# Second layers ahead of slot 3's sums, both transposes ahead of slot 5's placements, and loads of x early in a turn of a graph layer

## The chip, the cores and the metric

The kernel runs on one core of one Trainium2 chip. The metric is the device time of one execution in microseconds (us). The engines have their own instruction lists and meet through semaphores: PE (TensorE, matrix products; PEld is its weight load), DVE (VectorE), ACT (ScalarE), POOL (GpSimd) and SP (SyncE, which here only issues DMA transfers). Each engine works its list in the order in which it is written.

## The reference

One layer of a graph network on 12500 nodes with 128 features and 412500 edges with 48 attributes, whose receivers `dst` are sorted. All in float32.

```python
h   = max(layernorm(x), 0)                          # 12500 x 128
agg = segment_sum(edge_attr_48, dst, 12500)         # 12500 x 48
u   = graph_globals[0]                              # one row, the same for each node
hid = relu(concat([h, agg, u], axis=1) @ W1 + b1)   # 12500 x 256
out = x + hid @ W2 + b2                             # 12500 x 128
```

## The kernel before

The edges come in twelve turns of 33792 edges (and a rest), eleven groups of four chunks of 768 edges each. The groups of a turn lie in six slots of buffers `e0` to `e5` (`SLOTS`: two groups in a slot, one in slot 4). In the same turn 1024 nodes are worked on, as two blocks A and B of 512 (indices 0 and 1).

The steps, by the names in the code:

- Sums (`sums`, names `su0` to `su5`, L804): for each chunk PE multiplies the edges' attributes by a one-hot matrix `oh` that DVE makes from the receivers (`onehots`, L748). Results go to the PSUM banks `S0` (slots 0, 2, 4) and `S1` (slots 1, 3, 5). ACT copies them out (`ss0` to `ss5`, L808). So slot 5's sums may begin only when `ss3` has read `S1`.
- Placements (`place`, `pc0` to `pc4`, L826; `place_ends`, `pc5`, L788): PE adds a group's sums to the windows of the banks `ax` and `ay`, with one-hot matrices `pl`, `pln`, `plf` from DVE (L754, L767).
- Norm: DVE makes statistics of x for A and B (`stats`, L834) and the variance (`variance`, L839 to L844), ACT the root (`root`, L848), DVE its reciprocal and the shift (`shift`, L853 and L854), ACT the normed x (`norm`, four pieces a block, `xn0.0` to `xn1.3`, L860).
- Turn of a block (`turn`, `tu0` and `tu1`, L869): PE transposes the normed block into the bank `pt` or `po`; ACT copies it to `hta` or `htb` (`hT0`, `hT1`, L870).
- First layer (`layer_x` L879, `layer_e` L884, four products each), and `relu` on ACT (L889) into `hida` and `hidb`. It stands at the end of a turn.
- Second layer (`second`, `w20` for A and `w21` for B, L910; before, six of B's eight products stand apart as `second_begun`, L904). It works in the next turn on what `relu` left. Then DVE adds x and b2 into the output held in SBUF (`ho0`, `ho1`, L914; `hold`), and makes x + b2 of the present block (`add_b`, L864).
- Loads: e by SP (`load_e`), x by ACT (`load_x`), which refills the one buffer of a block for the next turn. The held outputs are stored at the end of the kernel.

The order of the work is written out by hand in `body`; each engine's list is that order, restricted to the engine. `Flow.order` finds the waits from what each step reads and writes. On PE the first turn skips the second layers, which have no input yet (`f.brief`): PE then waits for the weights and raises the semaphores of the skipped steps. PE's loop of code is cut at `f.mark`.

Of the kernel before, what the change touches and what calls it, by code (L numbers as in the profile page):

```python
# [18 lines left out]
P = 128  # L19
# [7 lines left out]
IN = 1024  # L27
BN = 512
R = 4
# [452 lines left out]
def kernel(  # L482
# [18 lines left out]
    NIT = E // IE  # L501
# [18 lines left out]
    def bank(name):  # L520
        return psum.tile([P, BN], F32, name=name)
# [4 lines left out]
    ph = [bank("ph0"), bank("ph1")]  # L526
    po = bank("po")
# [65 lines left out]
    f = Flow(nc, tc)  # L593
    op = f.op
    A, B, Z = 0, 1, 2
# [37 lines left out]
    def rows_of(ap, i, a, m, r):  # L633
        return span(ap, i, a, m * r).rearrange("(p r) d -> p (r d)", r=r)

    def load_x(k, a, m=P, eng="ACT"):
        r = RR[k]
        dv = xt[k].rearrange("p r d -> p (r d)")
        q = m - m % 16
        dma(eng, f"lx{k}", [], [f"x{k}"], dv[:q], lambda i: rows_of(x, i, a, q, r))  # L640
        if q < m:
            dma(eng, f"lx{k}t", [], [f"x{k}t"], dv[q:m], lambda i: rows_of(x, i, lambda i: a(i) + q * r, m - q, r))
# [78 lines left out]
    def cols(ap, i, a, n):  # L721
        return ap[:, ds(a(i), n)] if not isinstance(i, int) else ap[:, a(i):a(i) + n]
# [33 lines left out]
    def onehots(s):  # L756
        g = SLOTS[s]
        onehot(s, oh[s], ["rel_i"], rel_i[:, g[0] - 1:g[0]] if len(g) == 1 else rel_i[:, g[0] - 1:g[1]:g[1] - g[0]])
# [16 lines left out]
    def place_ends(sides):  # L775

        todo = []
        for side in sides:
            sv, pv, some = ((ss[5], pln, near), (ssf, plf, far_))[side]
            c = 0  # L780
            for j, frm, w, bk, at in some:
                todo.append((-w, side, sv[:, j], pv[:, c:c + w], bk, at, w))
                c += w
        todo.sort(key=lambda v: (v[0], 1 - v[1]))
        fresh = sides == (1,)
        op("PE", "pc5" + "f" * fresh, [v for side in sides for v in (("ss5", "pln"), ("ssf", "plf"))[side]],
           [f"bk{b}" for b in sorted({v[4] for v in todo})], lambda i: [
            nc.tensor.matmul(agg[bk][HI * bk:HI * bk + DE, at:at + w], sv, pv, start=fresh and n == 0, stop=True, skip_group_check=True)  # L788
            for n, (_, _, sv, pv, bk, at, w) in enumerate(todo)], late={"ss5": 1} if 0 in sides else None)
# [24 lines left out]
    def place(s, fresh=(), part=None):  # L814

        groups, sv, pv = SLOTS[s], ss[s], pl[s]
        todo = [(n, j) + v for j, g in enumerate(groups) for n, v in enumerate(pieces(g)) if part is None or v[0] == part]
        todo.sort(key=lambda v: v[2] if len(groups) == 1 else (v[0] if v[1] == 0 else 1 - v[0], v[1]))
        seen = set()

        def emit(i):
            seen.clear()
            out = []
            for _, j, bk, at, frm, w in todo:
                h = HI * bk
                out.append(nc.tensor.matmul(agg[bk][h:h + DE, at:at + w], sv[:, j], pv[:, j, frm:frm + w],  # L826
                                            start=bk in fresh and bk not in seen, stop=True, skip_group_check=True))
                seen.add(bk)
            return out
        op("PE", f"pc{s}" + ("" if part is None else f".{part}"), [f"ss{s}", f"pl{s}"], [f"bk{b}" for b in sorted({v[2] for v in todo})], emit)  # L830

    def stats(k, m=P):
        c = k % 2 * R
        op("DVE", f"st{k}", [f"x{k}", f"x{k}t"], [f"st{k}"], lambda i: [nc.vector.bn_stats(st[k // 2][:m, c + r], xt[k][:m, r]) for r in range(RR[k])])  # L834
# [15 lines left out]
    def shift(n, m=P):  # L850
        s = sm[n][:m]
        f.chain("DVE", f"sh{n}", [f"sm{n}a"], [f"sc{n}", f"sh{n}"],
            lambda: nc.vector.reciprocal(sc[n][:m], sc[n][:m]),  # L853
            lambda: nc.vector.scalar_tensor_tensor(sh[n][:m], s[:, 0], -0.5, sc[n][:m], OP.mult, OP.mult))  # L854

    def norm(k, some, m=P):
        n, c = k // 2, k % 2 * R
        for r in some:
            op("ACT", f"xn{k}.{r}", [f"x{k}", f"x{k}t", f"sc{n}", f"sh{n}"], [f"xn{k}"], lambda i, r=r: [
                nc.scalar.activation(xn[k][:m, r], xt[k][:m, r], AF.Relu, bias=sh[n][:m, c + r:c + r + 1], scale=sc[n][:m, c + r:c + r + 1])])  # L860

    def add_b(k, m=P, eng="DVE"):
        op(eng, f"xb{k}", [f"x{k}", f"x{k}t", "b2"], [f"xb{k}"], lambda i: [
            f.of[eng].tensor_tensor(xb[k][:m], xt[k][:m], b2_sb[:m, None, :].to_broadcast([m, RR[k], D]), OP.add)])  # L864

    def turn(k, m=P, bk=None, key="PT", eng="ACT"):
        pv = (pt if bk is None else bk)[:, :RR[k] * P].rearrange("p (r c) -> p r c", r=RR[k])
        copy = nc.scalar.copy if eng == "ACT" else nc.vector.tensor_copy
        op("PE", f"tu{k}", [f"xn{k}", "ident"], [key], lambda i: [nc.tensor.transpose(pv[:, r, :m], xn[k][:m, r], ident[:m, :m]) for r in range(RR[k])])  # L869
        op(eng, f"hT{k}", [key], [f"hT{k}"], lambda i: [copy(hT[k][:, :, :m], pv[:, :, :m])])  # L870
# [30 lines left out]
    def second_begun(k, bk, key, n):  # L901
        ov = bk.rearrange("p (r d) -> p r d", r=R)
        op("PE", f"w2{k}a", [f"hid{k}.{a}" for a in range(NH)] + ["w2"], [key], lambda i: [
            nc.tensor.matmul(ov[:, r], hid[k][:, a, r], w2[:, a], start=(a == 0), stop=(a == NH - 1)) for r in range(n) for a in range(NH)])  # L904

    def second(k, m=P, bk=None, key="PO", keep=None, begun=0):

        ov = (po if bk is None else bk)[:, :RR[k] * D].rearrange("p (r d) -> p r d", r=RR[k])
        op("PE", f"w2{k}", [f"hid{k}.{a}" for a in range(NH)] + ["w2"], [key], lambda i: [
            nc.tensor.matmul(ov[:m, r], hid[k][:, a, r, :m], w2[:, a], start=(a == 0), stop=(a == NH - 1)) for r in range(begun, RR[k]) for a in range(NH)])  # L910
        if keep is None:
            op("DVE", f"ot{k}", [key, f"xb{k}"], [f"ot{k}"], lambda i: [nc.vector.tensor_tensor(ot[k][:m], ov[:m], xb[k][:m], OP.add)])
        else:
            op("DVE", f"ho{k}", [key, f"xb{k}"] + (["spare"] if k == A else []), [f"hold{k}.{keep(f.at)}"], lambda i: [nc.vector.tensor_tensor(  # L914
                cols(hold[k], i, lambda i: keep(i) * (R * D), R * D).rearrange("p (r d) -> p r d", r=R), ov, xb[k], OP.add)])
# [90 lines left out]
    def body(it):  # L1006
        f.at = it

        def add_slots(*some):
            for s in some:  # L1010
                sums(s)
                if it < NIT - 1:
                    load_e(s, 1)

        keep = lambda i: (i + NIT - 2) % (NIT - 1)
        add_slots(0, 1)
        stats(A)
        farthest()
        fetch(1)
        add_slots(2)  # L1020
        stats(B)
        variance(0, (A, B))
        root(0)
        onehots(0)
        add_slots(3)
        shift(0)
        norm(A, (0,))
        add_slots(4)
        norm(A, (1, 2))
        onehots(1)  # L1030
        add_slots(5)
        norm(A, (3,))
        norm(B, range(R))
        onehots(2)
        onehots(3)
        place(0, (0, 1))
        for s in (1, 2, 3, 4):
            place(s)
        place_ends((0, 1))
        second(A, P, ph[A], "PH0", keep)  # L1040
        add_b(A)
        onehots(4)
        sums_out(A)
        sums_out(B)
        turn(A)
        second_begun(B, ph[B], "PH1", R - 1)
        if it < NIT - 1:
            load_x(A, lambda i: (i + 1) % NIT * IN)
        turn(B, P, po, "PO")
        second(B, P, ph[B], "PH1", keep, R - 1)  # L1050
        add_b(B)
        keep_ends()
        if it < NIT - 1:
            load_x(B, lambda i: (i + 1) % NIT * IN + BN)
        onehots(5)
        places_far()
        fetch_off(1)
        for s in (0, 1, 2, 3, 4):
            places(s)
        places_near()  # L1060
        layers(layer_x)
        layers(layer_e)
        layers(relu)
# [51 lines left out]
    f.at = NIT + 1  # L1115
    ends = [f"ot{k}" for k in range(3)] + [f"x{k}" for k in (A, B)] + [f"hold{k}.{j}" for k in (A, B) for j in range(NIT - 1)]
    op("SP", "end", [], ends, lambda i: [nc.sync.nop(nofuse=True)])
    f.mark, f.half, f.stops = "tu1", "of2", ("su1.b", "su1.c", "su2.b")
    f.brief, f.weights = ("w20", "w21a"), ("lw1h", "lw1a", "lw1b", "lw2")
    f.order((0, NIT - 1))  # L1120
    tc.mark_branch_hint_location("skip", engines=[ET.PE, ET.DVE])
    with tc.tile_critical(no_gpsimd_drain=True):
# [34 lines left out]
```

## Time and profile before

| | |
|---|---|
| device time, median of 3 runs | 259.55 us (259.35 to 259.8) |
| the profiled execution: time / span | 259.39 us / 257.5 us |
| PE busy | 238.0 us (92% of the span) |
| DVE busy | 231.3 us (90%) |
| ACT busy | 129.1 us (50%) |
| share of the chain that ended last: PE / DVE / DMA | 88% / 4% / 3% |
| HBM traffic | 94.33 MB, 366 GB/s over the span |

The span runs from the first to the last instruction. Busy time counts the instructions themselves; waits, branches and the issue of transfers do not count. A matmul of float32 shows as two records. Rows of the timeline begin with start and length in us; a bracket at a row's end names the idle time ahead of it and what ended it. In names, `out<-in` tells what is written and read, without buffer numbers: `s` is `S0` or `S1`, `ss` any of the six copies.

### The profile page before, as it was taken

How to read it: one execution, taken by the hardware profiler on the slowest of the kernel's cores; microseconds unless marked ns; L12 is line 12 of the kernel's file. 1: busy time of each engine (PE TensorE's matmuls, PEld its weight loads, DVE VectorE, ACT ScalarE, POOL GpSimd, SP SyncE). 2: the span in 40 equal slices, each digit the busy share in tenths (PEclk: the TensorE clock that was granted, in tenths of full speed). 3: DMA queues.
4: the chain of work that ended last, by engine and by line, in shares of the span. 5: the costliest groups of instructions: out<-in, count | busy, mean ns of one | idle time of the engine just before them, and what ended most of it. 6: DMA issues, size and time to landing. Idle time of an engine off the chain costs nothing.

```text
span 257.5 us, 17114 instructions
## 1 busy us (share of the span) xinstructions
PE 238.0 (92%) x7539; PEld 187.6 (73%) x7540; DVE 231.3 (90%) x572; ACT 129.1 (50%) x315; POOL 4.5 (2%) x18
## 2 busy tenths in 40 slices
PE   1778499999999999999999999999999999999990
PEld 1668374985976968949949869779589499598680
DVE  6489989989999999999999999999999999999840
ACT  5421273563654735825835646447258358356530
POOL 5000000000000000000000000000000000001000
PEclk9999869999999999999999999999999999999998
DMA  6999999999999999999999999999999999968972
GB/s 201 341 388 386 362 387 392 380 390 393 385 390 393 390 392 391 390 393 387 391 393 389 390 393 389 391 390 390 391 389 390 393 390 391 392 242 313 378 269 65
DMA packets 79508, 94.33 MB, mean 366 GB/s; under 512 B 3227, under 2 KB 72797, under 8 KB 79494
## 3 DMA queue, kind: packets, MB, share of 16 engines
q1 hardware_dynamic: 76086, 88.06, 95.7%
q10 hardware_dynamic: 3312, 6.03, 6.1%
q8 instruction: 7, 0.11, 0.2%
q0 software_dynamic: 96, 0.07, 0.1%
q14 instruction: 7, 0.06, 0.1%
HBM read 87.75 MB, written 6.40 MB: 366 GB/s over the span
## 4 chain that ended last, share of the span: by engine, by line
PE 88%; DVE 4%; DMA 3%; issue 1%; ACT 1%; SPq 0%; ACTq 0%; DVEq 0%
PE s L804 27%; PE ph L910 12%; PE ph L879 8%; PE ax L826 7%; PE ph L904 6%; PE pt L884 5%; PE pt L879 4%; PE ph L884 4%; PE po L879 4%; DMA holda<-in_dst_dram 3%; PE po L869 2%; PE pt L869 2%; PE ax L788 2%; DVE oh L748 1%; DVE pl L754 1%
## 5 line engine op out<-in xcount | busy, mean ns | idle before, releaser
L748 DVE TENSOR_TENSOR oh<-iota_v,rel_i 128x1344 f32<-128x1344 f32 (+1 forms) x78 | 109.7, 1435 | 0.0
L804 PEld LDWEIGHTS s<-e,oh 128*28 128x28 f32 x6336 | 73.3, 109 | 16.5 <-issue 12.0
L804 PE MATMUL s<-e,oh 128*28 128x48 f32 x6336 | 77.0, 210 | 6.1 <-issue 2.5
L889 ACT ACTIVATE hida<-pt,bias 128x512 f32<-128x512 f32 x12 | 8.2, 687 | 50.2 <-PE pt L884 50.2
L860 ACT ACTIVATE xna<-xa,shab,scab 128x128 f32<-128x128 f32 x48 | 23.7, 493 | 13.2 <-DVE shab L854 12.8
L808 ACT COPY ss<-s 128x96 f32<-128x96 f32 (+1 forms) x72 | 16.4, 228 | 24.6 <-PE s L804 24.6
L754 DVE TENSOR_SCALAR pl<-iota_w,off_i 128x186 f32<-128x186 f32 x117 | 27.6, 311 | 0.4
L910 PE MATMUL ph<-w,hida 128*128 128x128 f32 x192 | 24.6, 281 | 0.0
L860 ACT ACTIVATE xnb<-xb,shab,scab 128x128 f32<-128x128 f32 x48 | 23.5, 490 | 1.2
L910 PEld LDWEIGHTS ph<-w,hida 128*128 128x128 f32 x192 | 22.3, 191 | 0.6
L826 PE MATMUL ax<-pl,ss 128*48 128x186 f32 (+1 forms) x120 | 20.9, 324 | 0.0
L826 PE MATMUL ay<-pl,ss 128*48 128x186 f32 (+1 forms) x120 | 20.9, 324 | 0.0
L826 PEld LDWEIGHTS ax<-pl,ss 128*48 128x48 f32 x120 | 14.5, 129 | 4.1
L904 PE MATMUL ph<-w,hidb 128*128 128x128 f32 x132 | 16.5, 275 | 0.0
L904 PEld LDWEIGHTS ph<-w,hidb 128*128 128x128 f32 x132 | 15.6, 192 | 0.0
L826 PEld LDWEIGHTS ay<-pl,ss 128*48 128x48 f32 x120 | 14.5, 129 | 0.0
L884 PE MATMUL pt<-ags,w1a 48*128 48x512 f32 x24 | 13.5, 641 | 0.0
L884 PE MATMUL po<-ags,w1a 48*128 48x512 f32 x24 | 13.5, 641 | 0.0
L914 DVE TENSOR_TENSOR holdb<-ph,xbb 128x512 f32 x12 | 8.3, 692 | 5.6 <-PE ph L910 5.6
L879 PE MATMUL pt<-hta,w1h 128*128 128x512 f32 x24 | 12.4, 598 | 0.2 <-ACT hta L870 0.2
L884 PE MATMUL ph<-ags,w1a 48*128 48x512 f32 x48 | 12.3, 589 | 0.0
L879 PE MATMUL ph<-hta,w1h 128*128 128x512 f32 x24 | 12.3, 592 | 0.0
(151 smaller groups left out, 332.1 us busy)
## 6 DMA issues: line engine op xcount, KB each, us to landing
e<-in_edge_attr_dram SPq DMA_DIRECT2D x133, 576.0 KB, 8.8
xa<-in_x_dram ACTq DMA_DIRECT2D x11, 256.0 KB, 5.4
xb<-in_x_dram ACTq DMA_DIRECT2D x11, 256.0 KB, 5.3
out_dram<-holda SPq DMA_DIRECT2D x11, 256.0 KB, 3.3
out_dram<-holdb SPq DMA_DIRECT2D x11, 256.0 KB, 3.4
holda<-in_dst_dram SPq DMA_DIRECT2D x4, 384.0 KB, 5.8
e<-in_edge_attr_dram SPq DMA_DIRECT2D x1, 720.0 KB, 5.9
xa<-in_x_dram SPq DMA_DIRECT2D x1, 256.0 KB, 6.6
```

Of the source, the lines that this page charges most:

```text
L748: op("DVE", f"oh{name}", reads + ["iota_v"], [f"oh{name}"], lambda i: [nc.vector.tensor_tensor(ov, iota_v[:, None, None, :].to_broadcast([ ...
L754: nc.vector.tensor_scalar(out[:, j], iota_w, o[j], None, OP.is_equal) for j in range(len(o))])
L804: nc.tensor.matmul(S[k][NV * c:NV * c + V, j * DE:(j + 1) * DE], o[:, (j * CG + c) * T + t], ev[:, j * CG + c, t * DE:(t + 1) * DE], start ...
L808: op("ACT", f"ss{name}", [f"S{k}"], [f"ss{name}"], lambda i: [nc.scalar.copy(sv.rearrange("p j d -> p (j d)"), S[k][:, :m * DE])])
L826: out.append(nc.tensor.matmul(agg[bk][h:h + DE, at:at + w], sv[:, j], pv[:, j, frm:frm + w], start=bk in fresh and bk not in seen, stop=Tr ...
L860: nc.scalar.activation(xn[k][:m, r], xt[k][:m, r], AF.Relu, bias=sh[n][:m, c + r:c + r + 1], scale=sc[n][:m, c + r:c + r + 1])])
L869: op("PE", f"tu{k}", [f"xn{k}", "ident"], [key], lambda i: [nc.tensor.transpose(pv[:, r, :m], xn[k][:m, r], ident[:m, :m]) for r in range( ...
L879: nc.tensor.matmul(o, w1h[:, a * P:(a + 1) * P], hT[k][:, :, :m], start=first, stop=False, skip_group_check=True)])
L884: nc.tensor.matmul(o, w1a[h:h + DE, a * P:(a + 1) * P], ag[k // 2][h:h + DE, :, :m], start=False, stop=True, skip_group_check=True)])
L904: nc.tensor.matmul(ov[:, r], hid[k][:, a, r], w2[:, a], start=(a == 0), stop=(a == NH - 1)) for r in range(n) for a in range(NH)])
L910: nc.tensor.matmul(ov[:m, r], hid[k][:, a, r, :m], w2[:, a], start=(a == 0), stop=(a == NH - 1)) for r in range(begun, RR[k]) for a in ran ...
L914: op("DVE", f"ho{k}", [key, f"xb{k}"] + (["spare"] if k == A else []), [f"hold{k}.{keep(f.at)}"], lambda i: [nc.vector.tensor_tensor(cols( ...
```

## The change

In `body` the second layers of both blocks move from the placements to the place between slot 2's and slot 3's sums, in one piece each. With them the holds and x + b2 move. Half of A's norm moves ahead of slot 3's sums, the loads of x ahead of slot 5's sums (A) and behind B's norm (B). Both turns stand ahead of slot 5's placements. PE's loop is cut at `tu0` instead of `tu1`.

```diff
         farthest()
         fetch(1)
         add_slots(2)
+        onehots(0)
+        second(A, P, ph[A], "PH0", keep)
         stats(B)
         variance(0, (A, B))
         root(0)
-        onehots(0)
+        add_b(A)
+        shift(0)
+        norm(A, (0, 1))
+        second(B, P, ph[B], "PH1", keep)
+        add_b(B)
         add_slots(3)
-        shift(0)
-        norm(A, (0,))
+        norm(A, (2, 3))
+        onehots(1)
         add_slots(4)
-        norm(A, (1, 2))
-        onehots(1)
+        if it < NIT - 1:
+            load_x(A, lambda i: (i + 1) % NIT * IN)
+        norm(B, (0,))
         add_slots(5)
-        norm(A, (3,))
-        norm(B, range(R))
-        onehots(2)
-        onehots(3)
+        norm(B, (1, 2, 3))
+        if it < NIT - 1:
+            load_x(B, lambda i: (i + 1) % NIT * IN + BN)
+        for s in (2, 3, 4):
+            onehots(s)
         place(0, (0, 1))
         for s in (1, 2, 3, 4):
             place(s)
+        turn(A)
+        turn(B, P, po, "PO")
         place_ends((0, 1))
-        second(A, P, ph[A], "PH0", keep)
-        add_b(A)
-        onehots(4)
         sums_out(A)
         sums_out(B)
-        turn(A)
-        second_begun(B, ph[B], "PH1", R - 1)
-        if it < NIT - 1:
-            load_x(A, lambda i: (i + 1) % NIT * IN)
-        turn(B, P, po, "PO")
-        second(B, P, ph[B], "PH1", keep, R - 1)
-        add_b(B)
         keep_ends()
-        if it < NIT - 1:
-            load_x(B, lambda i: (i + 1) % NIT * IN + BN)
         onehots(5)
...
-    f.mark, f.half, f.stops = "tu1", "of2", ("su1.b", "su1.c", "su2.b")
-    f.brief, f.weights = ("w20", "w21a"), ("lw1h", "lw1a", "lw1b", "lw2")
+    f.mark, f.half, f.stops = "tu0", "of2", ("su1.b", "su1.c", "su2.b")
+    f.brief, f.weights = ("w20", "w21"), ("lw1h", "lw1a", "lw1b", "lw2")
```

What that makes of the engines' lists, at three places. First ACT, from slot 2's copy to slot 5's; before (in the brackets the steps waited for: `sm0_2_1` the variance, `sh0_1` the shift, `su3` slot 3's sums):

```order
L808 COPY ss_103<-s_65 128x96 [waits su2_b]
L848 ACTIVATE scab<-smab,eps 128x8 [waits sm0_2_1]
L808 COPY ss_104<-s_66 128x96 [waits su3]
L860 ACTIVATE xna<-xa,shab,scab 128x128 [waits sh0_1]
L808 COPY ss_105<-s_65 128x48 [waits su4]
L860 ACTIVATE xna<-xa,shab,scab 128x128 [waits xn0_0]
L860 ACTIVATE xna<-xa,shab,scab 128x128 [waits xn0_1]
L808 COPY ss_106<-s_66 128x96 [waits su5]
```

and after:

```order
L808 COPY ss_103<-s_65 128x96 [waits su2_b]
L848 ACTIVATE scab<-smab,eps 128x8 [waits sm0_2_1]
L860 ACTIVATE xna<-xa,shab,scab 128x128 [waits sh0_1]
L860 ACTIVATE xna<-xa,shab,scab 128x128 [waits xn0_0]
L808 COPY ss_104<-s_66 128x96 [waits su3]
L860 ACTIVATE xna<-xa,shab,scab 128x128 [waits xn0_1]
L860 ACTIVATE xna<-xa,shab,scab 128x128 [waits xn0_2]
L808 COPY ss_105<-s_65 128x48 [waits su4]
L241 COMPARE_AND_BRANCH
L600 ISA
L600 DMA xa<-in_x_dram 128x512 [waits xn0_3]
L239 UNCONDITIONAL_BRANCH
```

The copy of slot 3 (`ss_104`) stood ahead of the norms and stands now behind two of them; the load of x for A stands among the norms.

Next DVE, from the refill of the receivers (`rel_i`) to the shift; before:

```order
L733 TENSOR_SCALAR rel_i<-rel 128x264
L834 BN_STATS stab<-xb 128x6 [waits lx1]
L834 BN_STATS stab<-xb 128x6 x3
L839 TENSOR_TENSOR smab<-stab 128x16 [waits st1]
L841 TENSOR_TENSOR smab<-stab 128x8
L843 TENSOR_TENSOR smab<-smab 128x8 [waits sm0_1]
L844 SCALAR_TENSOR_TENSOR smab<-smab 128x8 [waits sm0_2_0]
L748 TENSOR_TENSOR oh_87<-iota_v,rel_i 128x1344 [waits su0]
L853 RECIPROCAL scab<-scab 128x8 [waits sq0]
L854 SCALAR_TENSOR_TENSOR shab<-smab,scab 128x8 [waits sh0_0]
```

and after:

```order
L733 TENSOR_SCALAR rel_i<-rel 128x264
L748 TENSOR_TENSOR oh_87<-iota_v,rel_i 128x1344 [waits su0,fr]
L914 ISA
L914 TENSOR_TENSOR holda<-ph_70,xba 128x512 [waits w20]
L834 BN_STATS stab<-xb 128x6 [waits lx1]
L834 BN_STATS stab<-xb 128x6 x3
L839 TENSOR_TENSOR smab<-stab 128x16 [waits st1]
L841 TENSOR_TENSOR smab<-stab 128x8
L843 TENSOR_TENSOR smab<-smab 128x8 [waits sm0_1]
L844 SCALAR_TENSOR_TENSOR smab<-smab 128x8 [waits sm0_2_0]
L864 TENSOR_TENSOR xba<-xa,b_sb 128x512
L853 RECIPROCAL scab<-scab 128x8 [waits sq0]
```

Hold A, which waits for PE's second layer of A (`w20`), now stands ahead of B's statistics.

Last PE, from the end of slot 2's sums to slot 5's; after (before, the four rows from L262 to the second layers were not there, and the rest stood in the same row; `lw2` and its neighbours are the loads of the weights, waited for in the first turn only):

```order
L804 MATMUL s_65<-e_76,oh_89 28x48 x12
L262 COMPARE_AND_BRANCH
L322 UNCONDITIONAL_BRANCH [waits lw2,lw1h,lw1a,lw1b]
L910 MATMUL ph_70<-w_141,hida 128x128 x8
L910 MATMUL ph_71<-w_141,hidb 128x128 x8
L257 UNCONDITIONAL_BRANCH
L804 MATMUL s_66<-e_77,oh_90 28x48 [waits le3_0,oh3,ss1]
L804 MATMUL s_66<-e_77,oh_90 28x48 x23
L804 MATMUL s_66<-e_77,oh_90 28x48 [waits le3_1]
L804 MATMUL s_66<-e_77,oh_90 28x48 x23
L804 MATMUL s_65<-e_78,oh_91 28x48 [waits le4_0,oh4,ss2]
```

The second layers moved from behind slot 5's placements to this place.

## The prediction

> **What bounds the kernel now.** I read the page's engine totals first, then the busy slices and the chain that ended last, then the busy time turn by turn, the waits, and at last the timeline of one turn in the middle.
>
> ```profile
> span 257.5 us, 17114 instructions
> PE 238.0 (92%) x7539; PEld 187.6 (73%) x7540; DVE 231.3 (90%) x572; ACT 129.1 (50%) x315; POOL 4.5 (2%) x18
> ...
> PEclk9999869999999999999999999999999999999998
> ...
> PE 88%; DVE 4%; DMA 3%; issue 1%; ACT 1%; SPq 0%; ACTq 0%; DVEq 0%
> ```
>
> PE is nearly the whole chain, and its granted clock (in tenths, slices of 6.4 us) is low only around 26 to 39 us. The busy time of each turn says it more sharply (columns: stretch, its length, then busy time of PE, PEld, DVE, ACT, POOL, the granted clock, DMA share, GB/s):
>
> ```profile
> 44.24:62.13 17.89, 17.89 (x619) 14.08 (x622) 16.75 (x41) 9.77 (x25) 0.00 (x0) 1.00 1.08 387
> ...
> sum 197.32, PE 197.25 PEld 154.43 DVE 188.60 ACT 108.51 POOL 0.73; mean PE 17.93 PEld 14.04 DVE 17.15 ACT 9.86 POOL 0.07
> ```
>
> The first row is the second turn (the first turn ends at 44.24), the sum is over all eleven turns after the first. PE has 0.07 us of idle time in 197.32 us. So a turn lasts as long as PE's instructions, 197.32 / 11 = 17.94 us, and there is nothing in these turns for a new order to win on PE; it can only add waits. DVE has 0.8 us of slack a turn, ACT 8 us. What PE waited for lies in the first turn:
>
> ```profile
> PE s L804 <- issue: 2.5, 2, 1.6
> ...
> PE s L804 <- ACT ss L808: 2.0, 1, 2.0
> ...
> PE s L804 <- DMA e<-in_edge_attr_dram: 1.6, 2, 0.9
> ```
>
> The middle row is the key to this case. In the timeline of the first turn:
>
> ```profile
> 29.53 0.30 ACT L848 ACTIVATE scab<-smab,eps 128x8 f32<-128x8 f32 x1 [4.83 <-DVE smab L844]
> 29.74 0.22 ACT L808 COPY ss<-s 128x96 f32<-128x96 f32 x1
> 30.01 0.96 PE L804 MATMUL s<-e,oh 128*28 128x48 f32 x44 [2.00 <-ACT ss L808]
> ```
>
> The copy of slot 3's sums (`ss3`) stood on ACT behind the square root, and that waited 4.83 us for DVE; slot 5's sums write the bank that `ss3` reads, so PE stood for 2.0 us until the copy was done. The change builds this situation into every turn.
>
> **The change, part by part.** One steady turn before, with the rows that price the steps; below, times are counted from the turn's first sum at 133.82.
>
> ```profile
> 133.82 6.14 PE L804 MATMUL s<-e,oh 128*28 128x48 f32 x528
> ...
> 136.16 0.86 DVE L834 BATCH_NORM_STATS2 stab<-xb 128x6 f32<-128x128 f32 x4
> ...
> 137.65 1.55 DVE L748 TENSOR_TENSOR oh<-iota_v,rel_i 128x1344 f32<-128x1344 f32 x1
> ...
> 139.12 0.20 DVE L853 RECIPROCAL scab<-scab 128x8 f32<-128x8 f32 x1
> ...
> 139.55 0.49 ACT L860 ACTIVATE xna<-xa,shab,scab 128x128 f32<-128x128 f32 x1 [1.08 <-DVE shab L854]
> 139.89 0.36 PE L826 MATMUL ax<-pl,ss 128*48 128x186 f32 x1
> 139.95 0.18 ACT L808 COPY ss<-s 128x48 f32<-128x48 f32 x1
> 140.07 1.02 ACT L860 ACTIVATE xna<-xa,shab,scab 128x128 f32<-128x128 f32 x2
> 141.35 0.28 PE L788 MATMUL ax<-plf,ssf 128*48 128x140 f32 x1
> 141.53 2.06 ACT L860 ACTIVATE xnb<-xb,shab,scab 128x128 f32<-128x128 f32 x4
> 141.63 0.21 PE L788 MATMUL ax<-plf,ssf 128*48 128x46 f32 x1
> 141.77 2.05 PE L910 MATMUL ph<-w,hida 128*128 128x128 f32 x16
> 143.66 0.60 PE L869 MATMUL pt<-ident,xna 128*128 128x128 f32 x4
> 143.86 0.69 DVE L914 TENSOR_TENSOR holda<-ph,xba 128x512 f32 x1
> 144.10 1.50 PE L904 MATMUL ph<-w,hidb 128*128 128x128 f32 x12
> 144.59 0.69 DVE L864 TENSOR_TENSOR xba<-xa,b_sb 128x512 f32<-128x512 f32 x1
> 144.66 0.59 ACT L870 COPY hta<-pt 128x512 f32<-128x512 f32 x1
> 145.31 0.34 ACTq L600 DMA_DIRECT2D xa<-in_x_dram  x1
> 145.44 0.60 PE L869 MATMUL po<-ident,xnb 128*128 128x128 f32 x4
> 146.32 1.02 PE L879 MATMUL pt<-hta,w1h 128*128 128x512 f32 x2
> 151.77 0.53 PEld L804 LDWEIGHTS s<-e,oh 128*28 128x28 f32 x44 [0.76 <-issue]
> ```
>
> *PE's work* is the same: sums 6.07 (133.82 to 139.89, eleven halves of 0.55), placements of slots 0 to 4 1.46 (139.89 to 141.35), slot 5's 0.42, block A's second layer 1.89, each turn 0.44, block B's second layer 1.79 (twelve of its sixteen records in 1.34), both first layers 5.45 (146.32 to 151.77). What is added are changes between kinds of matmul. From the last narrow placement at 141.63 to the first second-layer matmul pass 0.14, of which I take 0.1 for the change of kind. A turn has four such borders before (sums to placements, placements to second layer, into the first layers' part on the sums over edges, and back to sums) and eight after (both ends of the second layers, both ends of slot 5's placements more), so 0.4 at most; a border that falls into a wait costs nothing, and no border can give time back. TensorEngine Tiling (Array Packing) of the Trainium skill (Key Properties) says that a change of tiling mode drains the engine; it gives no price, and the 0.14 above agrees with it.
>
> *Slot 3's copy, the main term.* The second layer of A begins after six halves of sums, at 3.3; hold A begins 2.09 later (141.77 to 143.86), at 5.4. On DVE the statistics of B now stand behind hold A: they begin 0.66 later, at 6.06 (hold 0.69, neighbours overlapping a little). From there 1.49 to the instruction behind the variance (136.16 to 137.65), which is now the 0.69 of `xba` in place of 1.55, so 0.61 to the reciprocal (1.47 before), and 0.43 to the first norm of A (139.12 to 139.55): 8.59 against 5.73 before. Two norms of A now stand ahead of `ss3`: the second at 9.11 (0.52 on), the copy 0.40 later (as 139.55 to 139.95), at 9.51, and 0.27 from copy to sum (29.74 to 30.01): slot 5's sums begin at 9.78. PE is there at 3.3 + 1.89 + 1.79 + 0.1 + three halves 1.65 = 8.73. PE waits 1.05.
>
> *The turns.* After slot 5's sums (1.1) and the placements (1.46) and a border PE is at turn A at 12.44 and through at 12.88. Turn B needs the last norm of B. ACT: third and fourth norm of A from 9.63 to 10.64; then the load of x for A, which now stands between the norms and waits for the fourth (0.34, to 11.0; before, it ran beside a copy); four norms of B in 2.06: 13.1. PE waits 0.2. Then turn B 0.44, border, slot 5's placements 0.42, border: 14.16. The copy `hta` stands behind the second load of x (13.1 + 0.34 + 0.59 = 14.03) and is just in time. With 5.45 the turn ends at 19.61: 1.7 more than before. The sums of it: wait 1.05, wait 0.2, borders 0.4.
>
> Between bounds: without the load's 0.34 and with free borders it is 1.1 (the wait alone); if every copy on ACT between norms costs its full 0.2 and each border twice as much, 2.4. I take 1.7, from the rows nearest to the steps.
>
> *What is hidden.* Hold B's wait on PE vanishes, but DVE is off the chain. Loads of e for slots 3 to 5 are issued up to 5 us later in the turn; slot 5's at 10.9, and with the longest time to landing, 10.3, they are there at 21.2, 8 us ahead of their use in the next turn (19.61 + 9.78):
>
> ```profile
> DMA to landing us min/median/max: 5.6/8.7/10.3
> ```
>
> Less traffic a microsecond helps them; the x loads have a whole turn. If that cover went, PE would show waits on e.
>
> *The first turn.* The skipped second layers now stand ahead of slot 3, and with them the wait for the weights, of which the last is issued and lands so:
>
> ```profile
> 25.39 0.43 SPq L600 DMA_DIRECT2D w<-in_L_gnn_W_dram  x1
> ...
> DMA to landing us min/median/max: 6.2/6.2/6.2
> ```
>
> So slot 3's sums begin at 31.6, and hold A too. Slot 5's sums follow 4.4 later (9.78 less 5.4), at 36.0. PE's clock is low then, as it was after the earlier idle time (busy time of PE, granted clock):
>
> ```profile
> 29.00:30.00 1.00, 0.00 (x0) 1.00 1.12 336
> 30.00:31.00 1.00, 0.96 (x44) 0.64 1.05 327
> ...
> 36.00:37.00 1.00, 1.00 (x12) 0.50 1.05 370
> 37.00:38.00 1.00, 1.00 (x10) 0.94 1.08 382
> ```
>
> Half clock lasted until 37.1, that is 7.1 us after work resumed at 30.0; here until 38.7. So slot 5's sums take 2.3 and end at 38.3, the norms of B at 40.1, the first layers begin at 41.6 and end at 47.0 where it was 44.24: 2.8. Bounds: with the clock back ahead of slot 5's sums (1.1 in place of 2.3) and their copy 1.8; with the placements at half clock too (1.46 more) 4.2. TensorE: Matmul & The Clock Gate of the Trainium skill (Part 1) has the clock back after about 3.4 us of sustained work; by that the sum below would be 279.9. The 7.1 us are of this kernel, with gaps in its work, so I keep 2.8.
>
> *Sum.* 11 x 1.7 = 18.7, and 2.8: 21.5 on the profiled execution's 259.39 (span 257.5 and 1.9 around it), 280.9. It stands 0.16 under the median of 259.55, which is nothing here. The epilogue keeps its order.
>
> **The rivals.** *The clock falls in every turn.* PE's new waits could bring the half clock of the first turn into each. For it: after the 2.0 us without work the clock stood at half. Against it: the wait of 1.6 us (the longest under "issue" above) lies in the prologue ahead of the first low digit of the clock, and the new waits are shorter. 7.1 us at half clock cost 3.5: 259.4 + 2.8 + 11 x 5.2 = 319. The page on the clock gate in the Trainium skill (Part 1) has it fall after an idle window of about 3.4 us, and no wait here is that long.
>
> *Only the borders cost.* If `ss3` were there in time, 259.4 + 11 x 0.4 + 2.8 = 266.6. For it: ACT is half idle. Against it: it works its list in order, as the first turn shows.
>
> *Not slower, since DMA sets the pace.* DMA is never idle in a turn (share 1.08, 387 GB/s). If PE were stretched to the loads' pace while it looks busy, waits of PE would be absorbed as long as they stay under its hidden slack; x loads that leave the end of the turn would then be a small gain or none: 259. It decides from a slack of 1.7 a turn on. Against it: no wait of PE on e after the first turn, and PE's records lie back to back at full clock.
>
> **How the numbers follow.** Forecast 0.85: 281, its own range by the bounds: 259.4 + 11 x 1.1 + 1.8 = 273 to 259.4 + 11 x 2.4 + 4.2 = 290. Borders only 0.06, clock 0.05, DMA's pace 0.04 (half of it faster, half the same). A difference of 0.2% either way, 0.5 us, is about what a measurement of this kernel can tell. Slower 0.96, same 0.02, faster 0.02. The range leaves out the three rivals, 0.15.
>
> **What the changed profile would show.** A wait of PE at L804 on ACT's `ss` in each turn, about 1 us long; a small one at `po` L869 on `xnb`; turns of 19.6 us; norms of A beginning 3 us later in a turn; DVE waiting at hold A for `ph`; DMA under 387 GB/s; the first turn's sums of slot 3 after 31 us. I am wrong if `ss3` is read before slot 5 comes up, or if the clock column shows less than 1.00 in the later turns.

## The result, and the profile after

The changed kernel takes 285.46 us (median of 4 runs, 285.28 to 285.52) against 259.45 for the kernel before beside it: 1.0998 of its time, 95% interval 1.0984 to 1.1011. It is slower by 26.0 us.

The page of the changed kernel, the rows that answer to those of before:

```profile
span 283.8 us, 17108 instructions
...
PE 247.6 (87%) x7535; PEld 189.3 (67%) x7536; DVE 231.4 (82%) x572; ACT 128.5 (45%) x315; POOL 4.5 (2%) x18
...
PEclk9998559999999999999999999999999999999999
...
PE 55%; ACT 14%; DVE 13%; SPq 8%; issue 4%; DMA 2%; ACTq 1%; PEldq 0%
```

PE was 88% of the chain that ended last and is 55% now; ACT, DVE and SP's queue have taken most of the rest. The waits (who waited for whom, total, times, longest):

```profile
DVE holda L914 <- PE ph L910: 25.3, 11, 2.5
...
PE s L804 <- ACT ss L808: 10.6, 12, 0.9
PE s L804 <- DMA w<-in_L_gnn_W_dram: 8.5, 1, 8.5
...
PE s L804 <- issue: 4.0, 2, 2.4
...
PEld po L869 <- ACT xnb L860: 3.0, 10, 0.3
```

DVE waits at hold A in each turn, PE at slot 5's sums in each turn, once for the weights, and its weight load a little at turn B. The busy time of one turn, and of all eleven after the first (same columns as before):

```profile
149.53:169.27 19.74, 18.79 (x614) 14.15 (x613) 17.14 (x43) 9.81 (x25) 0.00 (x0) 1.00 1.01 356
50.83:267.74 216.91, 206.39 (x6734) 155.61 (x6732) 186.89 (x442) 107.94 (x265) 0.72 (x1) 1.00 0.99 347
```

So the 26.2 us between the two spans divide into the first turn, 6.7 (the second begins at 50.83, before at 44.17), the eleven turns, 19.6 (216.91 against 197.32), and nothing in the epilogue. One turn on the timeline (its first sum at 149.53), with the steps of the forecast:

```profile
152.84 2.05 PE L910 MATMUL ph<-w,hida 128*128 128x128 f32 x16
...
154.93 0.69 DVE L914 TENSOR_TENSOR holda<-ph,xba 128x512 f32 x1 [2.29 <-PE ph L910]
155.54 0.86 DVE L834 BATCH_NORM_STATS2 stab<-xb 128x6 f32<-128x128 f32 x4
...
156.61 1.74 PE L804 MATMUL s<-e,oh 128*28 128x48 f32 x144
...
157.14 0.30 ACT L848 ACTIVATE scab<-smab,eps 128x8 f32<-128x8 f32 x1 [3.95 <-DVE smab L844]
...
158.05 1.02 ACT L860 ACTIVATE xna<-xa,shab,scab 128x128 f32<-128x128 f32 x2 [0.61 <-DVE shab L854]
...
158.98 0.22 ACT L808 COPY ss<-s 128x96 f32<-128x96 f32 x1
...
159.25 1.22 PE L804 MATMUL s<-e,oh 128*28 128x48 f32 x96 [0.90 <-ACT ss L808]
...
160.16 0.34 ACTq L600 DMA_DIRECT2D xa<-in_x_dram  x1
160.40 0.12 PEld L826 LDWEIGHTS ax<-pl,ss 128*48 128x48 f32 x1
...
162.67 0.66 PE L869 MATMUL po<-ident,xnb 128*128 128x128 f32 x4
...
163.72 1.13 PE L879 MATMUL pt<-hta,w1h 128*128 128x512 f32 x2
```

Hold A waits 2.29 us for the second layer with B's statistics behind it on DVE; the root waits 3.95 us for them on ACT; the norms, and `ss3` behind two of them, come so late that PE stands 0.90 us ahead of slot 5's sums.

### The profile page after: what moved, and what is told of

Read it like the earlier page. It is cut to its first block, busy times and chain, and to the rows that moved or that the text cites. A ratio compares the mean times of both kernels' runs of the same rounds, so it can differ in the third digit from the quotient of the medians.

```text
span 283.8 us, 17108 instructions
## 1 busy us (share of the span) xinstructions
PE 247.6 (87%) x7535; PEld 189.3 (67%) x7536; DVE 231.4 (82%) x572; ACT 128.5 (45%) x315; POOL 4.5 (2%) x18
## 4 chain that ended last, share of the span: by engine, by line
PE 55%; ACT 14%; DVE 13%; SPq 8%; issue 4%; DMA 2%; ACTq 1%; PEldq 0%
PE s L804 14%; PE ph L910 9%; SPq L600 8%; PE ph L879 7%; ACT xnb L860 7%; ACT xna L860 6%; PE pt L879 4%; PE pt L884 4%; PE ph L884 4%; PE po L879 4%; DVE stab L834 3%; DVE holda L914 3%; PE po L869 3%; DVE xba L864 3%; DMA w<-in_L_gnn_W_dram 2%
## 5 line engine op out<-in xcount | busy, mean ns | idle before, releaser
L748 DVE TENSOR_TENSOR oh<-iota_v,rel_i 128x1344 f32<-128x1344 f32 (+1 forms) x78 | 107.8, 1434 | 2.3 <-PE s L804 1.9
L804 PE MATMUL s<-e,oh 128*28 128x48 f32 x6336 | 80.7, 212 | 23.0 <-ACT ss L808 10.6
L804 PEld LDWEIGHTS s<-e,oh 128*28 128x28 f32 x6336 | 75.5, 111 | 34.7 <-issue 21.1
L914 DVE TENSOR_TENSOR holda<-ph,xba 128x512 f32 x12 | 8.3, 691 | 28.2 <-PE ph L910 25.3
L848 ACT ACTIVATE scab<-smab,eps 128x8 f32<-128x8 f32 x12 | 3.6, 302 | 53.2 <-DVE smab L844 53.2
L910 PE MATMUL ph<-w,hidb 128*128 128x128 f32 x192 | 23.4, 275 | 0.0
L910 PEld LDWEIGHTS ph<-w,hidb 128*128 128x128 f32 x192 | 22.4, 192 | 0.0
L879 PE MATMUL pt<-hta,w1h 128*128 128x512 f32 x24 | 13.5, 645 | 0.0
L884 PE MATMUL ph<-ags,w1a 48*128 48x512 f32 x48 | 12.3, 589 | 0.0
```

The lines of the kernel that those rows point to most:

```text
L748: op("DVE", f"oh{name}", reads + ["iota_v"], [f"oh{name}"], lambda i: [nc.vector.tensor_tensor(ov, iota_v[:, None, None, :].to_broadcast([ ...
L804: nc.tensor.matmul(S[k][NV * c:NV * c + V, j * DE:(j + 1) * DE], o[:, (j * CG + c) * T + t], ev[:, j * CG + c, t * DE:(t + 1) * DE], start ...
L879: nc.tensor.matmul(o, w1h[:, a * P:(a + 1) * P], hT[k][:, :, :m], start=first, stop=False, skip_group_check=True)])
L884: nc.tensor.matmul(o, w1a[h:h + DE, a * P:(a + 1) * P], ag[k // 2][h:h + DE, :, :m], start=False, stop=True, skip_group_check=True)])
```

## The experiments

Eight kernels ran; each is an edit of the changed kernel or of the kernel before. A table of what the traces gave (the second turn's start, the length of a later turn, the time):

| kernel | second turn begins | a later turn | time, us |
|---|---|---|---|
| before | 44.17 | 17.94 | 259.4 |
| changed | 50.83 | 19.75 | 285.46 |
| copy of slot 3 first | 49.86 | 19.73 | 284.52 |
| hold A late | 49.70 | 18.69 | 273.14 |
| weights early | 43.83 | 19.75 | 278.83 |
| three edits | 44.42 | 18.38 | 264.01 |
| two borders more | 44.97 | 18.67 | 267.07 |
| before, root late | 42.69 | 17.94 (the second 19.46) | 259.50 |
| before, no x | 43.88 | 17.90 (the second 17.76) | 260.36 |
| root late, no x | 43.40 | 17.91 (the second 17.78) | 260.52 |

**1. The copy of slot 3 ahead of the norms again.** What holds PE, the copy's place on ACT or the norms that come late?

```diff
-        norm(A, (0, 1))
         second(B, P, ph[B], "PH1", keep)
         add_b(B)
         add_slots(3)
+        norm(A, (0, 1))
         norm(A, (2, 3))
```

> The changed kernel, with slot 3's copy on ACT ahead of all norms of A again (one edit on ACT, nothing on DVE or PE). Theory (the norms are late because hold A stands ahead of B's statistics on DVE, and the chain runs through the norms to turn B): PE no longer waits ahead of slot 5's sums (0.90 us a turn in the changed kernel), but the last norm of B comes at the same time, so turn B takes over the wait; a turn stays within 0.2 us of 19.74, the time within 2 of 285.5, say 284.5. Rival (the copy's place behind two norms is the cost): 11 x 0.9 = 10 us less, 275.5.

Measured: 284.52 us, 1.0978 of before (1.0961 to 1.0995), as forecast. The waits of PE:

```profile
PE po L869 <- ACT xnb L860: 11.9, 11, 1.1
PE s L804 <- DMA w<-in_L_gnn_W_dram: 9.4, 1, 9.4
```

The wait at slot 5's sums is gone and stands at turn B, 1.08 a turn in place of 0.88; the turn is 19.73 in place of 19.75. The rival, that the copy's place itself costs 10 us, falls. It is where PE happened to meet the late norms first.

**2. Hold A behind the variance on DVE.** The lists of PE and ACT stay as in the changed kernel.

```diff
-        onehots(0)
-        second(A, P, ph[A], "PH0", keep)
+        second(A, P, ph[A], "PH0", keep, part=(0,))    # PE's products
         stats(B)
         variance(0, (A, B))
         root(0)
-        add_b(A)
+        onehots(0)
         shift(0)
+        second(A, P, ph[A], "PH0", keep, part=(1,))    # DVE's hold
+        add_b(A)
         norm(A, (0, 1))
```

> The changed kernel, with B's statistics, the variance and the shift on DVE ahead of hold A again (one edit on DVE; the lists of PE and ACT are unchanged, slot 3's copy still stands behind two norms). Theory: the norms of A begin 3 us earlier, PE's wait ahead of slot 5 goes, and what stays is the borders and perhaps 0.1 to 0.2 at turn B: turns of 18.4 to 18.6, 11 x 1.2 = 13 us less, 271 to 272. Rival (the copy's place is the cost whatever DVE does): 285.5. Rival (the moves on PE cost by themselves): 285.5.

Measured: 273.14 us, 1.0543 (1.0523 to 1.0563), 12.3 us less than the changed kernel; 1.1 more than forecast at the nearer end. PE does not wait for `ss` any more in the later turns, though the copy still stands behind two norms. The busy time of one turn (columns as before) and the steps in it; slots 3 to 5 are one run of sums (line numbers in this run are up to three higher):

```profile
105.74:124.44 18.70, 18.63 (x614) 14.13 (x612) 17.22 (x43) 9.82 (x25) 0.00 (x0) 1.00 1.06 375
```

```profile
110.38 1.02 ACT L860 ACTIVATE xna<-xa,shab,scab 128x128 f32<-128x128 f32 x2 [0.77 <-DVE shab L854]
...
111.15 0.69 DVE L917 TENSOR_TENSOR holda<-ph,xba 128x512 f32 x1 [0.80 <-PE ph L911]
...
112.83 2.81 PE L804 MATMUL s<-e,oh 128*28 128x48 f32 x240
```

The norms of A begin 4.64 us into the turn in place of 8.52. The larger part of a turn's loss, 1.06 of 1.81 us, is DVE's order: the hold that waits for PE ahead of the statistics. In this turn PE's steps can be read without the large wait. Of what is left over 17.94, 0.29 lies at turn B (0.73 from turn A's start to turn B's, where 0.44 is the work); the rest, 0.47, I put down to borders, which run 5 tests.

**3. The weights loaded ahead of slot 3's e.** The four loads of `w1h`, `w1a` (twice) and `w2` move in the prologue's list on SP.

```diff
             if s == 3:
                 dma("SP", "lb2", [], ["b2"], b2_sb, b2[None, :].to_broadcast([P, D]))
                 load_x(A, lambda i: 0, eng="SP")
                 load_x(B, lambda i: BN, eng="SP")
+                dma("SP", "lw1h", [], ["w1h"], w1h, W1[0:D])
+                dma("SP", "lw1a", [], ["w1a"], w1a[0:DE], W1[D:D + DE])
+                dma("SP", "lw1b", [], ["w1b"], w1a[HI:HI + DE], W1[D:D + DE])
+                dma("SP", "lw2", [], ["w2"], w2, W2.rearrange("(a p) d -> p a d", p=P))
...
         load_e(5, 1, 1)
-        dma("SP", "lw1h", [], ["w1h"], w1h, W1[0:D])
-        dma("SP", "lw1a", [], ["w1a"], w1a[0:DE], W1[D:D + DE])
-        dma("SP", "lw1b", [], ["w1b"], w1a[HI:HI + DE], W1[D:D + DE])
-        dma("SP", "lw2", [], ["w2"], w2, W2.rearrange("(a p) d -> p a d", p=P))
```

> The changed kernel, with the four loads of the weights issued ahead of slot 3's loads of e in the prologue (six us earlier on SP's queue); the turns are unchanged. Theory (the first turn's loss of 6.66 us is the wait for the weights, with the half clock and the code fetch behind it): slot 3's sums begin at about 27 in place of 32.3, slot 5's at about 33; the first turn ends 3 to 5 us earlier, 281 to 282.5. Rival (the first turn is held by something else, the late norms or e): within 0.5 of 285.5.

Measured: 278.83 us, 1.0757 (1.0734 to 1.078): 6.6 us less, more than forecast. The second turn begins at 43.83, so the whole loss of the first turn (6.66) came from the wait for the weights and what it dragged along; the turns after are unchanged at 19.75. Slot 5's sums begin at 32.76 in place of 36.10, and there is no pause within them:

```profile
31.56 1.02 ACT L860 ACTIVATE xna<-xa,shab,scab 128x128 f32<-128x128 f32 x2 [0.61 <-DVE shab L854]
...
32.76 2.14 PE L804 MATMUL s<-e,oh 128*28 128x48 f32 x96 [2.34 <-ACT ss L808]
```

In the changed kernel PE paused in these sums for 2.44 us after a packet of instructions (more on it below). Here such a packet begins at 30.17, and PE goes on 2.59 later; the wait for `ss3` covers most of that time.

**4. The kernel before, with the root behind slot 3's copy.** The wait of 2.0 us in the first turn of before gave the forecast its key; does removing it gain?

```diff
-        root(0)
         onehots(0)
         add_slots(3)
+        root(0)
```

> The kernel before, with the square root on ACT behind slot 3's copy (one edit on ACT). Theory (in the first turn PE waited 2.0 us since that copy stood behind the root, and lost up to 3.4 us more to the half clock that followed): slot 5's sums begin at about 28.5 in place of 30.0, the later turns are unchanged; 255 to 259, where it ends depends on whether the code fetch (seen as the pause of 0.87 us in slot 5's sums) takes the wait over. Rival (that fetch or the loads of e end the wait anyway): within 0.5 of 259.5.

Measured: 259.50 us, 1.0008 (0.9993 to 1.0023): the same, as the rival has it; the range of the theory, 255 to 259, was missed. In the trace the first turn ends 1.48 us earlier than in the trace of before, but the second takes 19.46:

```profile
48.21 0.71 PE L804 MATMUL s<-e,oh 128*28 128x48 f32 x48 [0.65 <-DMA e<-in_edge_attr_dram]
...
49.62 0.71 PE L804 MATMUL s<-e,oh 128*28 128x48 f32 x48 [0.70 <-DMA e<-in_edge_attr_dram]
```

PE waits 1.35 us for e there and is at 62.15 where before it was at 62.06: in this trace the loads of e had no time to spare. How much of the 1.48 us is due to the edit stays open; run 7 below has slot 5's sums of the first turn nearly as early without it.

**5. Three edits together:** those of runs 2 and 3, and both loads of x on ACT behind the copies of the transposes. PE's list is that of the changed kernel.

```diff
-        if it < NIT - 1:                          # ahead of norm(B, (0,))
-            load_x(A, lambda i: (i + 1) % NIT * IN)
-        if it < NIT - 1:                          # behind norm(B, (1, 2, 3))
-            load_x(B, lambda i: (i + 1) % NIT * IN + BN)
         turn(A)
         turn(B, P, po, "PO")
         place_ends((0, 1))
+        if it < NIT - 1:
+            load_x(A, lambda i: (i + 1) % NIT * IN)
+        if it < NIT - 1:
+            load_x(B, lambda i: (i + 1) % NIT * IN + BN)
```

> The changed kernel with three edits together: B's statistics and the shift ahead of hold A on DVE, the weights loaded early, and both loads of x on ACT behind the copies hta and htb. PE's list is that of the changed kernel. Theory (what is left of the loss then is the borders between kinds of matmul, 0.47 us a turn as read from the trace): turns of 18.4, the first turn ends at about 43.9 like before, 259.4 + 11 x 0.47 = 264.6. Rival (waits remain somewhere, or the loads of x cost nothing on ACT): 266.5 or more.

Measured: 264.01 us, 1.0164 (1.0131 to 1.0197), close to the forecast of 264.6. PE has no idle time in a turn, and the turn is 0.44 longer than 17.94:

```profile
117.94:136.31 18.37, 18.37 (x614) 14.11 (x612) 17.23 (x42) 9.88 (x25) 0.00 (x0) 1.00 1.07 381
```

Against run 2 the turn is 0.31 shorter: the loads of x among the norms had cost that. So the 1.81 us that a later turn lost divide into 1.06 for DVE's order (run 2), 0.31 for the loads of x, and 0.44 that stays with PE's list and shows as busy time.

**6. Two more borders.** The same matmuls as in run 5, slot 4's placement between the two turns.

```diff
-        for s in (1, 2, 3, 4):
+        for s in (1, 2, 3):
             place(s)
         turn(A)
+        place(4)
         turn(B, P, po, "PO")
```

> The kernel of the run with three edits, with slot 4's placement put between the two turns on PE: the same matmuls, two more changes between kinds of matmul in each turn. Theory (each change costs PE 0.10 to 0.14 us): 0.2 to 0.29 a turn, 2.2 to 3.2 us over that kernel. Rival (borders are free, the 0.47 has another cause): within 0.5 of it.

Measured: 267.07 us, 1.0279 (1.0243 to 1.0315), 3.1 us over run 5. Again PE has no idle time:

```profile
119.64:138.30 18.66, 18.66 (x614) 14.00 (x612) 17.32 (x42) 9.98 (x25) 0.00 (x0) 1.00 1.05 373
```

0.29 a turn for two borders, 0.145 each, as the theory has it. A busy PE is not a PE at its peak: the same matmuls take longer when kinds of matmul alternate. What PE does in that time the records do not show.

**7 and 8. Without the loads of x in the turns,** from the kernel before and from run 4: `load_x` is left out of `body`, so each turn uses the first turn's x and 0.52 MB less a turn is moved.

> The kernel before without the loads of x inside the turns (x of the first turn is used throughout; this leaves out 0.52 of 7.01 MB a turn). Theory (PE's instructions set the turn, DMA at 390 GB/s is just enough): turns of 17.94 still, 259 to 259.5. Rival (DMA sets the turn's pace and PE is stretched to it): up to 1.3 us a turn less, 245 to 250.

> The kernel before with the root behind slot 3's copy, without the loads of x inside the turns (left out as in the run above). With the loads that edit brought the first turn's end 1.5 us forward and PE then waited 1.35 us for e in the second turn. Theory (DMA at its ceiling took the gain back): without the loads the gain stays, 1.2 to 1.6 us under the kernel before without loads, about 257.8. Rival (something else takes it back): the same time as that kernel.

Measured: 260.36 us (1.0037, 1.0024 to 1.0049) and 260.52 us (1.0035, 1.0015 to 1.0056). Turns of run 7:

```profile
115.35:133.25 17.90, 17.90 (x615) 14.12 (x613) 17.13 (x42) 9.87 (x25) 0.00 (x0) 1.00 1.03 363
```

With 7% less traffic a turn is 0.04 shorter, so PE sets the pace of the turns and not DMA; that rival falls. The time did not follow: from the start of the last addition to the end of the span it is 8.93 us (8.64 in run 8) where all the other kernels have 6.1, and the trace shows one more packet of instructions, at 258.47, in that stretch. Whether that packet is the cause was not tried.

Run 8 is no faster than run 7, so the 1.2 to 1.6 us were not seen. Its first turn ended 0.48 us ahead of run 7's, but it was 0.82 ahead already in slot 3's sums (24.77 against 25.59), where the edit has had no effect yet. And run 7, whose lists up to there are those of the kernel before, did not wait for `ss3` in its first turn. Its square root began at 28.15 where the trace of before has 29.53, and slot 5's sums began at 28.76, in run 4 at 28.66. So the wait of 2.0 us need not be in every execution of the kernel before. What run 4 is ahead of run 7 at the second turn (1.19) lies in the pause after the packet, 0.53 against 1.62, and run 8 with the same edit has 2.02 there: run 4's 1.48 us are not shown to come from the edit. That DMA took back a gain of run 4 is not shown: the second turn of runs 7 and 8 has no wait for e (17.76 and 17.78), but their first turns also ended later than that of run 4.

## Why the prediction was right, and what it missed

The forecast was 281, range 273 to 290; measured 285.46. The steps, in the order of the prediction:

- *The main term.* First norm of A at 8.59 by the sum, 8.52 measured (158.05 less 149.53); slot 5's sums at 9.78, measured 9.72; PE's wait 1.05, measured 0.90, and with the sums' new start after it 1.06 more in this part (3.79 from 156.61 to 160.40 against 2.73 in run 2). The chain named, PE's second layer, hold A, B's statistics, the root, the norms, the copy, is shown by run 2, which breaks it at hold A and nowhere else: 1.06 us a turn went with it, against the wait of 1.05 in the sum. PE waited at the place named, but run 1 shows that the copy behind two norms is not the cost: with the copy ahead of them the late norms hold PE at turn B, and the turn is as long.
- *The turns.* Turn B at 13.1, measured 13.14; first layers at 14.16, measured 14.19; the end at 19.61, measured 19.74. The difference lies in the last part: 5.55 where the sum had 5.45, a border at the first layers that was counted at 0.1 and costs twice, once in the gap and once in the first product (1.13 against 1.02). The borders together were put at 0.4 at most; run 5 shows 0.44. Turn B's wait was put at 0.2; taking the loads of x away gave 0.31. The eleven turns: 18.7 forecast, 19.6 measured.
- *The first turn* is the term that was mis-sized: 2.8 forecast, 6.66 measured, 4.2 the upper bound. The steps up to slot 5's sums held (hold A at 31.6 by the forecast, 31.78 measured; slot 5's sums at 36.0, 36.10 measured). Then two things came that the sum did not have: a pause in slot 5's sums, and a longer half clock.

```profile
36.10 0.36 PE L804 MATMUL s<-e,oh 128*28 128x48 f32 x2 [0.66 <-ACT ss L808]
...
38.90 2.14 PE L804 MATMUL s<-e,oh 128*28 128x48 f32 x94 [2.44 <-issue]
...
40.97 0.54 PE L826 MATMUL ax<-pl,ss 128*48 128x186 f32 x1
```

The pause is 2.44 us in which PE waited for nothing that the profile shows. In the trace a packet of 16 KB on the instruction queue begins at 36.35, and PE goes on 2.55 later. The kernel before has the same: packet at 29.31, PE on at 31.84, 2.53 later. There 0.70 of it lay under the wait for `ss3` and 0.96 under 44 records of sums, and 0.87 was seen, which the forecast did not count. The half clock lasted to 43.6 and not to 38.7, so the placements ran at half speed too: 2.8 (40.97 to 43.79) where 1.46 was counted. The pause and the longer half clock make nearly all of the 3.9 us that are missing (6.66 less 2.8); the upper bound of 4.2 had the half clock on the placements, but not the pause. The trace of before held both. From slot 5's first sum to the second turn it shows 14.16 us (30.01 to 44.17), the changed kernel 14.73, and the forecast gave 11.0. That stretch of before, set whole behind 36.0, gives a loss of 6.0.

Half-clock stretches here are of 3.4, 6.8, 10.2 and 17.1 us in the ten traces: whole numbers of a step of 3.4. TensorE: Matmul & The Clock Gate of the Trainium skill (Part 1) has the clock judged in free-running windows of about 3.4 us, and the steps agree with it. In such steps the clock came back behind one that PE worked through: from 40.18 to 43.59 in the changed kernel, where PE had been busy for only 2.45 and 1.28 us of the two steps before, and from 33.70 to 37.12 in the kernel before, after a step with 2.54. How much pause a step may hold is not settled: in run 5 one with 2.54 us of work (16.66 to 20.07) was enough. So the forecast's other number, 7.1 us taken from before, was no constant: it ran from PE's restart to the end of the first step without a long pause.

- *The rivals.* The clock stood at 1.00 in all later turns: no fall in every turn. The argument that no wait is as long as 3.4 us does not carry this, though. In the kernel before the clock fell at 30.29, when PE had worked 0.99 of the last 3.41 us and had been idle for 2.00 at the longest. In the later turns of the changed kernel PE was busy for 95% of the time and waited 0.9 at the longest. "Only the borders cost" is what run 5 had to be built for, 264.0 against the 266.6 of that rival, which had the first turn's 2.8 in it. "DMA sets the pace" fell by run 7; PE did wait for e in the second turn of run 4, where the first had ended 1.48 us earlier.

None of the kernels run here is faster than the kernel before.

## What to carry to other kernels

When one engine has no idle time, a new order can gain on it only what busy time it saves, and may cost some (run 6): price the change by that and by what it delays on the others. Look for an instruction that waits and is put ahead of work that other engines need; each engine works in order, so everything behind it is late by the whole wait, and the stall shows up wherever the bound engine meets the late work first. Removing the place where it shows moves it on; removing the wait's cause removes it.

## What the runs showed of the hardware that was not expected

- Fetching code seems to stall PE. In the first pass through the loop all ten traces have a 16 KB packet on the instruction queue and PE's next start 2.33 to 2.61 us after the packet's begin, within slot 5's sums or at their start. Not each such packet does: behind the next one of the changed kernel, at 42.68, PE has no pause. This is read from the traces and was not tried by itself.
- A change between full and narrow matmuls costs PE 0.145 us here, and the records show it as busy time (run 6).
- The granted clock changes in steps of 3.4 us. In the changed kernel it stayed at half for 17.1 us, of which PE waited for the weights in the first 5.8; in the other 11.3 PE worked, with pauses of 0.66 and 2.44 us.
